# A convolution block with a pooled gate: the gate's second product on VectorE, and the order of work at two stage seams

## The chip, the cores and the metric

The kernel runs on one core of a Trainium2 chip, as one launch. The metric is the device time of the launch in microseconds (us), taken as the median of several runs. Besides, one execution was recorded by the hardware profiler; all views of the profile come from that one.

## The reference, cut to what matters

The input is x, 16 images of 192 channels and 64 by 64 pixels, in fp32. Layer 0 is a convolution block, layer 1 a convolution whose taps depend on the image:

```
h     = layernorm over channels(x)
p, g  = split(conv1x1(h))                       # 192 + 192 channels
p     = depthwise 3x3(p)
mixed = (four directional scans(p) + depthwise 3x3(p)) * sigmoid(g)
mixed = gelu(batchnorm over images and pixels(mixed))
x     = x + conv1x1(mixed)
x     = x + fc2(gelu(fc1(layernorm(x))))        # 192 -> 768 -> 192

t     = mean over pixels(x) @ w1.T              # squeeze: 192 -> 48
t     = relu(gamma * (t - running_mean) * rsqrt(running_var + 1e-5) + beta)
taps  = t @ w2.T + b2                           # excite: 48 -> 192 x 9, of which 4 are kept by a mask
out   = per image and channel 3x3 convolution(x, taps) + bias
```

## The kernel before

The work goes through three stages, each over all images, and every engine's instructions run in the order in which the program writes them (a manual schedule). Most tiles hold two images: image 0 on partitions 0 to 63, image 1 on 64 to 127, with the 192 channels as three tiles t of 64.

**Stage one** (loop over n, eight parts for each of eight image pairs; `project`, `turn`, `variance`) normalises x and projects it. A part has four groups of 128 pixels of each image; four parts fill a block, whose results lie in an SBUF buffer (`stg` for even blocks, `mid` for odd ones). VectorE takes image 0's projection out of PSUM (L520), ScalarE image 1's (L521). The block before is stored by DMA while the next is computed: `store_first` (L530) copies the first group of eight channels by DMA straight into `pg_even`, a part of the SBUF tile `low`, and `store` puts the rest into DRAM (`pg_d`), from the SP and POOL queues. Small preparations are hung beside certain parts n with `beside`, among them `squeeze_scale` (n = 50) and the loads of the later weights (`load_weights`, n = 40 to 44). After the loop, L595 and L596 store the last block's first group and part 0.

**Stage two** (L768, loop over k, one channel of each half at a time, groups of four k's) works on one group of eight channels after the other. Iteration k issues, in this order: the decay tables of k + 1 on ScalarE (`tables`), the vertical products and the gate of k - 1 (`vertical`, `gate`), loads for later groups, the scans of k + 1 on VectorE (`scans`), the depthwise products of k + 2 (`depthwise`), and the local products and sigmoid of k (`local`, `sigmoid`). Iterations -2 and -1 fill the pipeline. In iteration -2 also stands `hidden_bias` (L138): 18 products of one column that add fc1 applied to the second layernorm's bias onto fc1's own bias `bf1`. Its weights `wf1` are scaled by `scale_hidden` in iterations 1, 3 and 5.

**The seam behind stage two** (L801 to L807): `keep_up(4)` and `keep_up(1)` are products whose result nobody reads, which fill TensorE's time; `spread` and `batch_norm` make the batch statistics from VectorE's per-channel statistics; `turn_back` transposes the first mixed chunk for stage three.

**Stage three** (L1257, loop over n, 64 chunks of 512 pixels of an image pair, eight chunks per pair) does the output projection, the MLP and the dynamic convolution. fc2 is computed in seven partial products over halves (`seven`, called by `second`); `first` does fc1 and ScalarE its GELU. Chunk n also prepares chunks n + 1 and n + 2. When a pair has ended (`ended`, at the first chunk of the next one), `pooled` sums what the additions into the image have accumulated. `squeeze` (L1112) then multiplies by `w1t` (three products, 48 outputs for the two images) and applies the batch norm and the relu on VectorE (`red`). Later in the same chunk `excite` (L1122) multiplies `red` by `w2t` with 24 products of one column into `ps_k`, and VectorE adds b2 (`taps`). In the profile each fp32 product is recorded as two, so these are 6 and 48 there. The taps then scale shifted images in `dynamic`: one ScalarE and three VectorE operations per piece, spread over the next chunks. The last pair's pieces follow the loop, as the tail (from L1344 on), partly as diagonal products on TensorE (`dynamic_last`). PSUM tiles of a name tag share a fixed number of buffers: "f1" has two, and holds fc1's results, the output projection's pair (`ps_o`), squeeze's result (`ps_t`) and two of fc2's partial sums (`ps_s`).

Two lines that a sentence doesn't say well, the layout of the pooled sums, in which each half has a column of its own and zeros in the other's, and excite's products:

```
nc.vector.tensor_reduce(pool2[q, :, i], s["sums"][q], AX.X, ALU.add)
both(pk[:, t, k], lambda i: w2t[:, k, 64 * t:64 * t + 64], lambda i: s["red"][:, i:i + 1], True, True)
```

Of the kernel before, what the change touches and what calls it, by code (L numbers as in the profile page):

```python
# [21 lines left out]
F32 = mybir.dt.float32  # L22
AF = mybir.ActivationFunctionType
ALU = mybir.AluOpType
# [31 lines left out]
def conv_block_kernel(ctx: ExitStack, tc: tile.TileContext, x, prm, w_in, w_out, w_fc1, b_fc1, w_fc2, w1, bn1, w2, out):  # L56
# [46 lines left out]
    w2t = k2.tile([RED, NTAP, C], F32, tag="w2t", name="w2t")  # L103
    b1 = k2.tile([RED, 4], F32, tag="b1", name="b1")
    s1 = k2.tile([RED, 1], F32, tag="s1", name="s1")

    mean64 = k2.tile([128, 64], F32, tag="mean64", name="mean64")

    def load_weights(k):

        if k == 0:
            nc.gpsimd.memset(mean64, 1.0 / C)
            nc.sync.dma_start(wo, w_out[0:128])
            for q in HALF:
                nc.sync.dma_start(wo2[q], w_out[128:C])
        elif k == 1:
            load_cls3(wf1, w_fc1)
        elif k == 2:
            nc.sync.dma_start(wf2, w_fc2.rearrange("(m p) c -> p m c", p=128))
        elif k == 3:  # L120
            nc.sync.dma_start(bf1, b_fc1)
            load_cls3(w1t, w1)
            nc.sync.dma_start(w2t, w2[:, 0:NTAP, :])
        else:
            nc.sync.dma_start(b1, bn1)
            nc.sync.dma_start(pv[:, 0], prm[0:128])
            for q in HALF:
                nc.sync.dma_start(pv[q, 1], prm[128:C])


    def squeeze_scale():
        nc.scalar.activation(s1, b1[:, 3:4], AF.Sqrt, bias=eps5[0:RED])
        nc.vector.reciprocal(s1, s1)
        nc.vector.tensor_mul(s1, s1, b1[:, 0:1])

        nc.vector.tensor_scalar_mul(w1t, w1t, 1.0 / NPIX)

# [28 lines left out]
    ones = ce.tile([128, 128], F32, tag="ones", name="ones")  # L166
    pv = ce.tile([128, 2, NPRM], F32, tag="pv", name="pv")
# [11 lines left out]
    mats[0]["lm"] = lm_even  # L179
    mats[1]["lm"] = mid[:, NPG:NPG + 5 * HW * (GC // 2)].rearrange("p (k m c) -> p k m c", k=5, m=HW)  # L180
# [69 lines left out]
    with ExitStack() as stage:  # L250
# [284 lines left out]

        def store(blk, d, queues):
# [58 lines left out]
        store_first(blk)  # L595
# [3 lines left out]
    with ExitStack() as stage:  # L599
# [168 lines left out]
        for k in range(-2, n_bp + 1):  # L768
            if 0 <= k + 1 < n_bp:
                tables(k + 1)  # L770
# [14 lines left out]
            if k == -2:  # L785
                hidden_bias(psb.tile([128, 2, CH], F32, tag="l", name="pb_h")[:, 0])
            if k + 2 < n_bp:
                depthwise(k + 2)
            if 0 <= k < n_bp:
                local(k)  # L790
                sigmoid(k)
            if k in (1, 3, 5):
                scale_hidden(k // 2)
            if k == n_bp - hp_:

                load_y(0, y_low, (nc.sync,), (0, 1))
# [4 lines left out]
        keep_up(4)  # L801
# [4 lines left out]
        batch_norm()  # L806
        turn_back(y_low, mxs[0], 0, 2)  # L807
# [304 lines left out]
    def squeeze(p):  # L1112
        s = pst[p]
        pt = ps2.tile([128, 2, CH], F32, tag="f1", name="ps_t", bufs=2)[:, 0]
        for t in range(3):
            nc.tensor.matmul(pt[0:RED, 0:2], w1t[:, t], pool2[:, t], start=(t == 0), stop=(t == 2))
        red = hp2.tile([RED, 2], F32, tag="red2", name="red2")
        nc.vector.tensor_scalar(red, pt[0:RED, 0:2], b1[:, 2:3], s1, ALU.subtract, ALU.mult)
        nc.vector.tensor_scalar(red, red, b1[:, 1:2], 0.0, ALU.add, ALU.max)
        s["red"] = red  # L1120

    def excite(p):  # L1122
        s = pst[p]
        pk = ps2.tile([128, 3, NTAP, 1], F32, tag="a", name="ps_k")
        for t in range(3):
            for k in range(NTAP):
                both(pk[:, t, k], lambda i: w2t[:, k, 64 * t:64 * t + 64], lambda i: s["red"][:, i:i + 1], True, True)
        taps = hp2.tile([128, 3, NTAP], F32, tag="taps", name="taps")
        nc.vector.tensor_add(taps, pk[:, :, :, 0], pt3[:, :, B2:B2 + NTAP])
# [127 lines left out]
    for n in range(n_ch + 1):  # L1257
# [79 lines left out]
        if ended is not None:  # L1337
            excite(ended)
            if ended < n_pairs - 1:
                pieces += [(ended, g, t) for g in range(NG) for t in range(3)]  # L1340
# [79 lines left out]
```

## Time and profile before

| what | us |
|---|---|
| three runs, median (lowest to highest) | 3562.65 (3562.14 to 3562.84) |
| the profiled execution's own time | 3559.31 |
| its span, first to last instruction | 3557.5 |
| TensorE busy (products) | 3525.5 |
| VectorE busy | 2741.6 |
| ScalarE busy | 1834.7 |
| GpSimd busy | 1155.7 |
| stage one ends on TensorE at | 591.2 |
| stage two's last products end at | 1261.4 |
| tail begins (last pair's squeeze) at | 3520.4 |

In the profile PE is TensorE's products, PEld its weight loads, DVE is VectorE, ACT ScalarE, POOL GpSimd and SP SyncE. A line such as "592.30 4.79 PE L141 MATMUL pb_h<-pt,wf 64*128 64x1 f32 x36 [1.10 <-ACT mid L521]" of the timeline gives the start and the length in us, the engine, the line of the kernel, the operation, what it writes and reads, the size of the weights (rows * columns), the size of the moving operand, the number of instructions, and in brackets how long the engine was idle before and what ended that. In the chain of waits a line gives start, length, engine, tile, line and number. PEclk is the share of TensorE's full clock that was granted. The mean of it is 0.995 over the span.

### The profile page before, as it was taken

The page shows a single profiled execution, that of the slowest core. Times are in us where ns is not written, and L with a number is a line of the kernel's source. Part 1 is how long each engine was busy: PE and PEld are TensorE (multiplying, and loading weights), DVE is VectorE, ACT ScalarE, POOL GpSimd, SP SyncE. Part 2 cuts the span into 40 slices and gives each one's busy share as a digit, 9 for nine tenths or more (in the row PEclk, how much of TensorE's full clock was granted, in tenths as well). Part 3 has the DMA queues.
Part 4 walks back from the last instruction along what each step waited for, and adds up shares of the span by engine and source line. Part 5 has one row for each costly group of instructions (what it writes and reads, how often), then busy time and mean ns, then how long its engine had stood idle before and what let it go on. Part 6 is the DMA issues. An engine that isn't in the chain of part 4 may idle for free.

```text
span 3557.5 us, 79074 instructions
## 1 busy us (share of the span) xinstructions
PE 3525.5 (99%) x33426; PEld 1874.6 (53%) x33426; DVE 2741.6 (77%) x4722; ACT 1834.7 (52%) x2067; POOL 1155.7 (32%) x1246
## 2 busy tenths in 40 slices
PE   9999999999999999999999999999999999999998
PEld 6666866555555544454444444444445444444443
DVE  7888776999999975557777776777677777767765
ACT  3444445888888844344444445454444444453543
POOL 3434342111111134333333333343433333343433
PEclk9999999999999999999999999999999999999999
DMA  7999998999999941112222222222222222232213
GB/s 177 263 272 264 271 294 282 282 301 283 280 282 286 247 123 34 40 54 60 69 71 70 67 65 81 58 75 62 80 60 69 68 74 62 68 82 58 75 34 90
DMA packets 288987, 492.29 MB, mean 138 GB/s; under 512 B 24816, under 2 KB 183016, under 8 KB 288632
## 3 DMA queue, kind: packets, MB, share of 16 engines
q1 hardware_dynamic: 246772, 341.85, 35.8%
q0 software_dynamic: 40928, 144.36, 14.2%
q8 instruction: 263, 4.31, 0.5%
q10 hardware_dynamic: 932, 1.03, 0.1%
q14 instruction: 92, 0.75, 0.1%
HBM read 284.95 MB, written 197.92 MB: 136 GB/s over the span
## 4 chain that ended last, share of the span: by engine, by line
PE 89%; DVE 1%; DMA 1%; issue 0%; ACT 0%; SPq 0%; ACTq 0%; POOL 0%; DVEq 0%
PE ps_f L997 28%; PE ps_f L852 19%; PE ps_l L674 11%; PE ps_pj L515 7%; PE ps_d L630 7%; PE ps_s L852 7%; PE ps_o L907 5%; PE ps_o L900 2%; PE ps_m L936 1%; PE ps_v L936 1%; PE ps_xt L486 1%; PE ps_k L852 0%; DMA pg_d<-mid 0%; DMA xa<-in_x_dram 0%; DMA mixed_d<-mid 0%
## 5 line engine op out<-in xcount | busy, mean ns | idle before, releaser
L997 PE MATMUL ps_f<-h,wf 64*64 64x512 f32 x9216 | 1014.9, 590 | 0.0
L999 ACT ACTIVATE gl<-ps_f,bf 128x1024 f32<-128x1024 f32 x384 | 427.8, 1114 | 1082.3 <-PE ps_f L997 1080.0
L997 PEld LDWEIGHTS ps_f<-h,wf 64*64 64x64 f32 x9216 | 346.2, 133 | 599.0 <-issue 575.1
L852 PE MATMUL ps_f<-gl,place 128*64 128x256 f32 (+1 forms) x3072 | 528.7, 486 | 1.1 <-ACT rs L979 1.1
L515 PE MATMUL ps_pj<-wi,xa 64*128 64x384 f32 x3072 | 520.1, 488 | 9.2 <-DVE stg L520 6.2
L515 PEld LDWEIGHTS ps_pj<-wi,xa 64*128 64x128 f32 x3072 | 334.0, 189 | 159.9 <-DVE stg L520 10.5
L1032 POOL TENSOR_TENSOR gl<-gl 128x512 f32<-128x512 f32 x192 | 308.6, 1634 | 159.2 <-PE ps_f L852 159.0
L852 PEld LDWEIGHTS ps_f<-gl,place 128*64 128x64 f32 x3072 | 225.2, 137 | 217.7 <-issue 145.8
L1022 POOL COPY turn<-o 128x1 f32<-128x1 f32 x84 | 16.4, 195 | 832.8 <-DVE o L65 832.8
L1028 POOL TENSOR_TENSOR t<-gl 128x512 f32<-128x512 f32 x192 | 246.0, 1281 | 89.0 <-ACT gl L999 44.6
L1030 POOL TENSOR_TENSOR t<-gl,t 128x512 f32<-128x512 f32 x192 | 247.0, 1287 | 44.2 <-ACT gl L999 30.8
L65 DVE SCALAR_TENSOR_TENSOR o<-ximg,taps,o 128x1024 f32<-128x1024 f32 x180 | 231.8, 1288 | 4.9
L473 POOL DMA_DIRECT2D xa<-in_x_dram x192 | 120.2, 634 | 323.8 <-PE ps_pj L515 277.1
L665 DVE TENSOR_TENSOR_SCAN v<-tab,q 128x1024 f32<-128x1024 f32 x96 | 218.3, 2274 | 7.8 <-ACT tab L653 7.8
L667 DVE TENSOR_TENSOR_SCAN v<-tab,q 128x1024 f32<-128x1024 f32 x96 | 217.5, 2266 | 0.0
L1055 DVE SCALAR_TENSOR_TENSOR ximg<-ps_f,pt,ximg 128x256 f32<-128x256 f32 (+1 forms) x176 | 96.6, 549 | 151.2 <-PE ps_f L852 151.2
L653 ACT ACTIVATE tab<-mask,dec_b 128x1024 f32<-128x1024 f32 x192 | 209.6, 1144 | 0.0
L521 ACT ACTIVATE mid<-ps_pj,rsa 128x384 f32<-128x384 f32 x128 | 119.5, 937 | 167.0 <-PE ps_pj L515 150.1
L521 ACT ACTIVATE stg<-ps_pj,rsa 128x384 f32<-128x384 f32 x128 | 119.2, 935 | 162.6 <-PE ps_pj L515 144.2
L913 DVE SCALAR_TENSOR_TENSOR ximg<-ps_o,pt,low 128x256 f32<-128x256 f32 x264 | 113.0, 478 | 93.0 <-PE ps_o L907 90.3
L907 PE MATMUL ps_o<-low,wo 128*64 128x256 f32 x1536 | 182.1, 385 | 0.4 <-ACT low L880 0.4
L493 DVE BATCH_NORM_STATS2 st<-ps_xt 128x6 f32<-128x192 f32 x512 | 171.7, 335 | 8.3 <-PE ps_xt L486 7.7
(258 smaller groups left out, 5604.0 us busy)
## 6 DMA issues: line engine op xcount, KB each, us to landing
low<-in_x_dram SPq DMA_DIRECT2D x128, 384.0 KB
out_dram<-o SPq DMA_DIRECT2D x172, 256.0 KB
mid<-pg_d SPq DMA_DIRECT2D x8, 4096.0 KB
low<-mixed_d SPq DMA_DIRECT2D x116, 256.0 KB
low<-pg_d SPq DMA_DIRECT2D x7, 4096.0 KB
pg_o<-pg_d SPq DMA_DIRECT2D x7, 4096.0 KB
xa<-in_x_dram POOLq DMA_DIRECT2D x192, 128.0 KB, 5.6
xa<-in_x_dram SPq DMA_DIRECT2D x192, 128.0 KB
```

What stands on the lines that cost most here:

```text
L65: nc.vector.scalar_tensor_tensor(o, in0, scalar, in1, ALU.mult, ALU.add, **kw)
L515: nc.tensor.matmul(ps[i], pixels(n, t, g)[q], wi[q, t].rearrange("p g k c -> p (g k c)"), start=(t == 0), stop=(t == 2))
L521: nc.scalar.activation(stag[blk][1][:, :, j], ps[1], AF.Copy, scale=rs[:, g, 1:2])
L630: nc.tensor.matmul(dst(ps[o, ih]), mats[g % 2]["dm"][q, di + 1, :, ch], src(s["pg"][q, :, 0, ch]), start=(di == 0), stop=stop)
L674: nc.tensor.matmul(dst(bst[k]["ps"][o, i]), lm_of(g)[q, m, :, c], src(q, ih), start=start, stop=stop)
L852: nc.tensor.matmul(ps[q], w(i), rhs(i), start=start, stop=stop, **kw)
L907: nc.tensor.matmul(ps[wh][q].rearrange("p (r w) -> p r w", w=32), wo[:, 64 * t:64 * t + 64], cols(rows(s["mx"][:, i]))[:, :, wh], start=fi ...
L997: nc.tensor.matmul(pf[o, i], wf1[q, t, m0:m0 + 64], s["h"][q, t], start=(t == 0), stop=(t == 2))
L999: nc.scalar.activation(gl, pf, AF.Gelu, bias=bf1[:, m:m + 1])
L1028: sub(t1[:, m], b12(m), b11(m))
L1030: sub(t2[:, m], b22(m), t1[:, m])
L1032: sub(b12(m), b22(m), b12(m))
```

## The change

Four things change:

- **Excite on VectorE.** `w2t` no longer is a tile of its own: it is loaded late (iteration 92 of stage two, by the POOL queue) into the buffer of the even groups' depthwise matrices, and at the seam behind stage two 24 products against an identity turn it into `w2x`, which has channels on the partitions and the 48 hidden values along the row (`taps_by_channel`; two ScalarE copies out of PSUM). One filler product of `keep_up(4)` goes. The batch norm of the squeeze is folded into `w1t` and a constant `c0` beforehand (four small VectorE operations in `squeeze_scale`, a product and two VectorE operations in `squeeze_rows` behind `batch_norm`). `squeeze` then makes, for each half, the hidden vector on all 64 partitions, with the pooled sum spread over 64 weight columns and `w1t` moving, six products; VectorE adds `c0`, multiplies relu of that by `w2x` over 576 elements, reduces them to 12 and adds b2. All of it stands where squeeze stood; `excite` is gone.
- **The last block's first group by engines.** Behind stage one's loop, `keep_first` copies it with two VectorE and two ScalarE instructions instead of four DMAs; three filler products of 384 columns stand before.
- **Tables first.** The decay tables of channel 0 are made in iteration -2 instead of -1, ahead of the first depthwise results on ScalarE.
- **The MLP bias** (`hidden_bias`) moves from iteration -2 to iteration 0, behind the local products, and uses a PSUM buffer of tag "d".

```diff
-    w2t = k2.tile([RED, NTAP, C], F32, tag="w2t", name="w2t")
+    w2x = k2.tile([128, 3, NTAP, RED], F32, tag="w2x", name="w2x")
+    c0 = k2.tile([128, RED], F32, tag="c0", name="c0")
...
             load_cls3(w1t, w1)
-            nc.sync.dma_start(w2t, w2[:, 0:NTAP, :])
...
         nc.vector.tensor_scalar_mul(w1t, w1t, 1.0 / NPIX)
+        nc.vector.tensor_mul(sq_s, b1[:, 2:3], s1)
+        nc.vector.tensor_sub(sq_s, b1[:, 1:2], sq_s)
+        for k, v in enumerate((s1, sq_s)):
+            nc.vector.tensor_scalar_mul(sq_d[:, k], ident[0:RED, 0:RED], v)
+
+    def squeeze_rows(pr):
+
+        nc.tensor.matmul(pr[:, 0:2 * RED], ones[0:RED], sq_d.rearrange("p k r -> p (k r)"), start=True, stop=True)
+        nc.vector.tensor_mul(w1t, w1t, pr[:, 0:RED].unsqueeze(1).broadcast_to([128, 3, RED]))
+        nc.vector.tensor_copy(c0, pr[:, RED:2 * RED])
+
+    def taps_by_channel(pk):
+
+        for t in range(3):
+            for k in range(NTAP):
+                j = (2 * t + k % 2) * RED
+                for q in HALF:
+                    nc.tensor.matmul(pk[q, k // 2, j:j + RED], w2t[:, k, 64 * t:64 * t + 64], ident[0:RED, 0:RED],
+                                     start=True, stop=True)
+        for h in range(2):
+            nc.scalar.activation(w2x[:, :, 2 * h:2 * h + 2], pk[:, h, 0:6 * RED].rearrange("p (t k r) -> p t k r", t=3, r=RED),
+                                 AF.Copy)
...
+    w2t = mats[0]["dm"][0:RED].rearrange("p k m c -> p (k m c)")[:, 0:NTAP * C].rearrange("p (k c) -> p k c", k=NTAP)
...
+        def keep_first(blk):
+
+            for i, par, q, i8, b, qh in each(blk):
+                o, a = pg_even[qh, i8 * NB + b].rearrange("p k c j -> p (k c) j"), stag[blk][i][q, 0:2 * GC]
+                if i == 0:
+                    nc.vector.tensor_copy(o, a)
+                else:
+                    nc.scalar.activation(o, a, AF.Copy)
...
-        store_first(blk)
+        warm_ = bank()
+        for _ in range(3):
+            nc.tensor.matmul(warm_[:, 0:2 * C], ident, wi[:, 0].rearrange("p g k c -> p (g k c)"), start=True, stop=True)
+        keep_first(blk)
         store(blk, 0, (nc.gpsimd, nc.gpsimd))
...
         for k in range(-2, n_bp + 1):
-            if 0 <= k + 1 < n_bp:
+            if k == -2:
+                tables(0)
+            elif 0 < k + 1 < n_bp:
                 tables(k + 1)
...
-            if k == -2:
-                hidden_bias(psb.tile([128, 2, CH], F32, tag="l", name="pb_h")[:, 0])
             if k + 2 < n_bp:
                 depthwise(k + 2)
             if 0 <= k < n_bp:
                 local(k)
                 sigmoid(k)
+            if k == 0:
+                hidden_bias(psb.tile([128, 2, CH], F32, tag="d", name="pb_h", bufs=2)[:, 0])
...
             if k == n_bp - hp_:
 
+                nc.gpsimd.dma_start(w2t, w2[:, 0:NTAP, :])
...
-        keep_up(4)
+        taps_by_channel(psb.tile([128, 2, CH], F32, tag="d", name="pk_h", bufs=2))
+        keep_up(3)
...
         batch_norm()
+        squeeze_rows(psb.tile([128, 2, CH], F32, tag="d", name="pr_h", bufs=2)[:, 0])
...
         for t in range(3):
-            nc.tensor.matmul(pt[0:RED, 0:2], w1t[:, t], pool2[:, t], start=(t == 0), stop=(t == 2))
-        red = hp2.tile([RED, 2], F32, tag="red2", name="red2")
-        nc.vector.tensor_scalar(red, pt[0:RED, 0:2], b1[:, 2:3], s1, ALU.subtract, ALU.mult)
-        nc.vector.tensor_scalar(red, red, b1[:, 1:2], 0.0, ALU.add, ALU.max)
-        s["red"] = red
-
-    def excite(p):
-        s = pst[p]
-        pk = ps2.tile([128, 3, NTAP, 1], F32, tag="a", name="ps_k")
-        for t in range(3):
-            for k in range(NTAP):
-                both(pk[:, t, k], lambda i: w2t[:, k, 64 * t:64 * t + 64], lambda i: s["red"][:, i:i + 1], True, True)
+            for i, q in enumerate(HALF):
+                nc.tensor.matmul(pt[q, 0:RED], pool2[q, t, i:i + 1].broadcast_to([64, 64]), w1t[q, t], start=(t == 0), stop=(t == 2))
+        red = hp2.tile([128, RED], F32, tag="red2", name="red2")
+        nc.vector.tensor_add(red, pt[:, 0:RED], c0)
+        prod = hp2.tile([128, 3, NTAP, RED], F32, tag="prod", name="prod", bufs=1)
+        flat = lambda a: a.rearrange("p t k r -> p (t k) r")
+        nc.vector.scalar_tensor_tensor(flat(prod), red.unsqueeze(1).broadcast_to([128, 3 * NTAP, RED]), 0.0, flat(w2x), ALU.max, ALU.mult)
         taps = hp2.tile([128, 3, NTAP], F32, tag="taps", name="taps")
-        nc.vector.tensor_add(taps, pk[:, :, :, 0], pt3[:, :, B2:B2 + NTAP])
+        nc.vector.tensor_reduce(taps.rearrange("p t k -> p (t k)"), flat(prod), AX.X, ALU.add)
+        nc.vector.tensor_add(taps, taps, pt3[:, :, B2:B2 + NTAP])
         s["taps"] = taps
...
-        if ended is not None:
-            excite(ended)
-            if ended < n_pairs - 1:
-                pieces += [(ended, g, t) for g in range(NG) for t in range(3)]
+        if ended is not None and ended < n_pairs - 1:
+            pieces += [(ended, g, t) for g in range(NG) for t in range(3)]
```

More of the change, by code (lines that the diff above doesn't have):

```diff
@@ L166, in conv_block_kernel @@
     ones = ce.tile([128, 128], F32, tag="ones", name="ones")
+    sq_s = ce.tile([RED, 1], F32, tag="sq_s", name="sq_s")
+    sq_d = ce.tile([RED, 2, RED], F32, tag="sq_d", name="sq_d")
     pv = ce.tile([128, 2, NPRM], F32, tag="pv", name="pv")
```

## The prediction

> **What bounds the kernel now.** I read the page first: busy time by engine, then the chain that ended last.
>
> ```profile
> PE 3525.5 (99%) x33426; PEld 1874.6 (53%) x33426; DVE 2741.6 (77%) x4722; ACT 1834.7 (52%) x2067; POOL 1155.7 (32%) x1246
> ```
>
> TensorE is busy for 99% of the span, so a change gains what it takes off TensorE, or what it takes out of the few places where TensorE waits or runs slowly. The change touches three such places. First, the ends of image pairs in the last stage, from the chain in order of time:
>
> ```profile
> 1533.89 5.31 PE ps_f L997 x48
> 1568.62 5.31 PE ps_f L997 x48
> 1605.25 5.31 PE ps_f L997 x48
> ```
>
> The same group of products starts every chunk. A plain chunk lasts 1568.62 - 1533.89 = 34.73 us, the chunk in which a pair has ended 1605.25 - 1568.62 = 36.63. So a pair's end costs 1.90 us of TensorE; there are seven inside the loop (chunks 8, 16 ... 56) and an eighth in the tail. The timeline of TensorE shows where it goes, a plain chunk first:
>
> ```profile
> 1554.23 4.04 PE L852 MATMUL ps_f<-gl,place 128*64 128x256 f32 x24
> 1558.10 1.47 PE L852 MATMUL ps_s<-t,ws 128*64 128x256 f32 x12
> ...
> 1586.32 0.39 PE L1116 MATMUL ps_t<-pool,w1t 128*48 128x2 f32 x5
> ...
> 1589.16 4.10 PE L852 MATMUL ps_f<-gl,place 128*64 128x256 f32 x24
> 1593.19 1.56 PE L852 MATMUL ps_k<-red,w2t 48*64 48x1 f32 x48
> 1594.68 1.52 PE L852 MATMUL ps_s<-t,ws 128*64 128x256 f32 x12
> ```
>
> From ps_f to ps_s it is 3.87 us plain and 5.52 at a pair's end: excite (ps_k) costs 1.65. The other 0.25 is squeeze (ps_t). VectorE beside it, in its timeline:
>
> ```profile
> 1587.29 0.92 DVE L913 SCALAR_TENSOR_TENSOR spare<-ps_o,pt,low 128x256 f32<-128x256 f32 x2
> ...
> 1590.74 0.48 DVE L1055 SCALAR_TENSOR_TENSOR spare<-ps_f,pt,spare 128x256 f32<-128x256 f32 x1 [2.48 <-PE ps_f L852]
> ```
>
> VectorE idles 2.48 us before L1055: room for more work there.
>
> Second, the seam of stages one and two, in TensorE's timeline and in the sums by stretch (columns: length, busy PE, PEld, DVE, ACT, POOL, then PEclk, DMA share, GB/s):
>
> ```profile
> 592.30 4.79 PE L141 MATMUL pb_h<-pt,wf 64*128 64x1 f32 x36 [1.10 <-ACT mid L521]
> 597.02 10.71 PE L630 MATMUL ps_d<-low,dm 64*64 64x512 f32 x120
> ```
>
> ```profile
> 592.24:595.65 3.41, 3.35 (x30) 3.36 (x31) 0.00 (x0) 0.00 (x0) 3.10 (x6) 1.00 0.49 124
> 595.65:599.06 3.41, 3.41 (x20) 2.18 (x23) 0.16 (x1) 0.00 (x0) 0.00 (x0) 0.50 0.98 290
> 599.06:602.48 3.42, 3.42 (x36) 1.79 (x32) 0.00 (x0) 0.00 (x0) 0.45 (x1) 0.50 1.08 381
> 602.48:605.89 3.41, 3.41 (x52) 2.00 (x48) 0.74 (x1) 3.36 (x5) 0.48 (x1) 1.00 1.12 379
> ```
>
> TensorE stops at 591.20, waits 1.10, computes the MLP bias (products of one column), and after 3.4 us of these the clock halves for 6.83 us, into the first depthwise.
>
> Third, the seam of stages two and three:
>
> ```profile
> 1261.39 3.70 PE L759 MATMUL ps_i<-wf,ident 128*128 128x512 f32 x8
> 1264.93 1.60 PE L734 MATMUL pm<-stats,ones 128*128 128x192 f32 x4
> ```
>
> ```profile
> 1268.08:1271.49 3.41, 2.80 (x23) 1.96 (x24) 2.56 (x7) 1.33 (x2) 0.00 (x0) 1.00 0.97 277
> 1271.49:1274.91 3.42, 3.04 (x10) 0.77 (x8) 3.38 (x4) 2.64 (x4) 0.00 (x0) 0.50 0.61 180
> ```
>
> The batch statistics (pm) start the moment four filler products (ps_i) are done, 0.05 us after VectorE's last statistics.
>
> **What the Trainium skill says.** "TensorE: Matmul & The Clock Gate", Part 1: the clock halves after an idle window of about 3.4 us and returns after a busy one, and the windows run freely. The trace agrees (3.41 us steps above) and adds that a window full of one-column products counts as idle; one with 1.3 us of full products in 3.41 (1268.08) did too. "VectorE: DVE Perf Modes", the perf-mode tier table and the errata section: fp32 tensor_tensor and tensor_reduce run at one element per cycle, (N+151)/0.96 ns. The trace: 128x512 took 0.69 us (formula 0.691), the 48-element reduce 0.20 (0.207). "ScalarE: Activation LUTs", What ACT_TABLE_LOAD costs: an ACTIVATE with immediate scale and bias takes 186 + 0.833 N ns; the trace has 0.47 for 256 elements with a bias operand, whose price there is 0.49. "DMA: Bandwidth & Descriptors", Anatomy of one DMA: about 2 us fixed; the last low<-mid stores landed in 2.0.
>
> **Part 1, excite on VectorE.** Removed per pair: 48 ps_k products, 1.65 us of TensorE. Squeeze grows from 6 products of 45 ns (0.25 us) to 12 on 64x64 quarters with 48 columns. The trace has no such product. Bounds: 31 ns (ps_k's 1.49/48) to 45 ns each, 0.37 to 0.54, so +0.12 to +0.29; I take +0.2. Added on VectorE: add from PSUM 0.25 (as L1118, 0.27), the 576-element product 0.84 (L65: 0.776 at 512, 1.288 at 1024, so 1.0 ns an element), the reduce 0.76 (estimate by the formula), the tap add 0.17: 2.0 us in place of 0.5. They start at about 1586.95 and end at 1589.0; queued behind on VectorE are L913 (0.92) and a memset (0.1), until 1590.0. L1055 can't start before 1590.74. So 0.7 us are spare: nothing on the path. Seven ends: 7 x (1.65 - 0.2) = **-10.15 us** (-9.5 to -10.7).
>
> In the tail it is a chain: ps_t at 3520.43 to taps done at 3523.32, 2.89 us. New: products 0.55, then 2.0 of VectorE and some 0.15 of hand-overs, 2.7: **-0.2** (-0.5 to +0.2).
>
> **Part 2, first seam.** Before, from 591.20 to the end of the first depthwise (ACT takes it at 602.50): 11.25 us. After: three fillers of 384 columns (ps_i: 0.885 for 512, so 0.66 each) 2.0 us to 593.2; in their shade the copies: ACT free at 592.24, two of 0.40 to 0.47, done by 593.2; VectorE free at 592.16, two of at most 0.42. Four DMA issues go from POOL's and SP's queues, so what stands behind them moves up by about 1 us. Then depthwise at full clock, 2.61 (later x40 groups): 4.6 us. The bias moves behind local products: 36 at 0.11 us (full clock, 30 in 3.35) are 4.0. Saved so far: 11.25 - 4.6 - 4.0 = 2.65. But the bias, wherever it stands, is a stretch of 4 us of one-column products. By my sum it runs from 603.7 to 607.7 (three depthwise and one local product group behind 593.2); on the trace's own grid the window 602.48 to 605.89 would then be 64% bias, more than the 61% or so of light work that halved the clock at 1271.49. I expect the clock to halve there for two windows, a loss of 3.41: 3.41 - 2.65 = **+0.75 us** (-2.65 if it stays full, +0.8 at worst). Tables first: the scan waited for ACT's table until 605.15, but VectorE was not the limit. Its gate for channel 1 came at 621.66, 2.75 us behind TensorE's 618.91, and at 1246.17 it is 0.13 behind, with no wait of TensorE between. So zero: what VectorE gains there only widens that slack, and without the slack it would be a gain. The bias add on VectorE (0.16) waits for TensorE, with gate 0 queued behind, which waits for later products anyway: zero. Group 1's load on POOL (issued 602.03, 13.8 to land, 615.8) feeds products that began at 618.73; it moves up by 1 us, they by at most 2.65: zero, with 1.2 spare.
>
> **Part 3, second seam.** taps_by_channel puts 48 products of 48 columns in place of one filler: 1.5 to 1.9 us for 0.885, and pm comes later by 0.6 to 1.0, on the path to the first GELU. I take +0.75. The two ACT copies out of PSUM (288 elements, 0.43 each) lie in ACT's 9.75 us of idle time; pm's buffer is free by then. squeeze_rows puts one product and 0.4 us of VectorE ahead of the last transpose (done 1272.57; ACT reads it at 1272.89): at most 0.1. The late w2 load stands in POOL's queue four channels (27 us) before use: zero. The half clock of 1271.49 to 1274.91 cost the first output products 0.93 (8 in 1.98, later 1.05); with everything shifted it may miss them. Half of that, -0.45: together **+0.3** (-0.2 to +1.1). In stage one, four small VectorE operations (0.15 to 0.2 each) join at 480 us; TensorE has two banks a side ahead: zero (to +0.7).
>
> **Sum**: -10.15 - 0.2 + 0.75 + 0.3 = -9.3 us against the profiled execution (span 3557.5, its own time 3559.31). The median of the runs, 3562.65, is 3.3 higher; I take the difference over: **3553.3 us**. A measurement can tell about 0.2% (7.1 us) from no change.
>
> **Rivals.** (a) The clock stays full at the first seam (the bias split between two windows): 2 to 3.4 us better, **3550.5**. For: windows run freely. Against: 4 us covers over 60% of some window in most positions. (b) The wait that takes the place: without ps_k, TensorE comes to ps_s at 1593.2, and if ps_s's banks were those of the output pair it would wait for VectorE's L913 until 1594.46; an end gains 0.25, less 0.2, and the total is +0.5: **3563**. Against: the trace's record of the first ps_s product waits on GpSimd alone, in both kinds of chunk, so it seems to have ps_t's banks. (c) Slower: VectorE's broadcast and reduce are slow, and TensorE waits at each pair's end. It decides once the VectorE line is longer than 0.5 + 2.48 = 3.0 us, and passes the gain at 4.45, that is near 2 us for each 576-element operation (3.5 ns an element; L65 has 1.0 to 1.3). At 4 ns, 5.1 us, it is 7 x 0.65 = 4.5 plus 0.85 from the tail and the seams, slower: **3568**. Against it: every row of fp32 VectorE work above.
>
> **Chances.** Forecast 0.60 (its own range 3551.5 to 3555.5), (a) 0.19, (b) 0.15, (c) 0.06. Faster by over 0.2% (below 3555.5): 0.60 x 0.97 + 0.19 = 0.77; within 0.2%: 0.17; slower 0.06. The range runs from (a)'s lower end, 3549.5, to 3558, where half of the hidden wait of (b) would lie.
>
> **What would show it.** Chunks at a pair's end of 35.2 us against 34.73; ps_s 3.9 us behind ps_f with no wait; VectorE's new line near 2.0 us. Depthwise from 593.2 at full clock, and half a clock near 606. pm near 0.7 us later after ps_l. I am wrong if pair ends stay near 36.6, or if the seams move by more than 3 us.

## The result, and the profile after

The changed kernel takes 3548.71 us (median of 5 runs, 3545.64 to 3550.64); the kernel before, on the same chip, 3562.84. The ratio is 0.9956, 95% interval 0.9942 to 0.9971: 14.1 us faster. The forecast was 3553.3 with a range from 3549.5 to 3558.0, so the sign was right, the gain half as large again as forecast, and the time just below the range. The profiled execution took 3545.64 us (span 3543.9), 13.7 less than the one of before.

The page's line of busy time, and the chain of waits at the same three chunks (start, length, tile):

```profile
PE 3512.8 (99%) x33144; PEld 1905.7 (54%) x33144; DVE 2754.9 (78%) x4738; ACT 1836.2 (52%) x2071; POOL 1156.8 (33%) x1245
```

```profile
1533.02 5.31 PE ps_f L1039 x48
1567.75 5.31 PE ps_f L1039 x48
1602.81 5.31 PE ps_f L1039 x48
```

A plain chunk still lasts 1567.75 - 1533.02 = 34.73 us. The chunk at a pair's end lasts 35.06, not 36.63: 1.57 less, and seven of them 11.0. TensorE's and VectorE's timelines in that chunk:

```profile
1585.34 0.51 PE L1159 MATMUL ps_t<-w1t,pool 64*64 64x48 f32 x12
...
1588.42 4.04 PE L894 MATMUL ps_f<-gl,place 128*64 128x256 f32 x24
1592.29 1.47 PE L894 MATMUL ps_s<-t,ws 128*64 128x256 f32 x12
```

```profile
1585.89 0.21 DVE L1161 TENSOR_TENSOR red<-ps_t,c 128x48 f32<-128x48 f32 x1 [4.68 <-PE ps_t L1159]
1586.13 0.87 DVE L1164 SCALAR_TENSOR_TENSOR prod<-red,w2x 128x576 f32<-128x576 f32 x1
1587.03 0.75 DVE L1166 TENSOR_REDUCE taps<-prod 128x12 f32<-128x576 f32 x1
1587.82 0.17 DVE L1167 TENSOR_TENSOR taps<-taps,pt 128x12 f32<-128x12 f32 x1
...
1589.93 0.49 DVE L1097 SCALAR_TENSOR_TENSOR spare<-ps_f,pt,spare 128x256 f32<-128x256 f32 x1 [1.06 <-PE ps_f L894]
```

From ps_f to ps_s it is 3.87 us, as in a plain chunk, and no wait stands before ps_s. VectorE's new line runs from 1585.89 to 1587.99, 2.1 us, and VectorE still idles 1.06 us before L1097. The first seam on TensorE, with the two stretches that matter (columns as before: length, busy PE, PEld, DVE, ACT, POOL, then PEclk, DMA share, GB/s):

```profile
587.03 2.20 PE L631 MATMUL pb<-wi,ident 128*128 128x384 f32 x6
589.34 8.30 PE L667 MATMUL ps_d<-low,dm 64*64 64x512 f32 x116
...
600.36 4.18 PE L163 MATMUL pb_h<-pt,wf 64*128 64x1 f32 x36
604.47 3.19 PE L711 MATMUL ps_l<-v,low 64*64 64x512 f32 x16
```

```profile
601.74:605.15 3.41, 3.41 (x34) 3.18 (x37) 1.53 (x2) 3.41 (x4) 0.00 (x0) 1.00 1.01 387
605.15:608.56 3.41, 3.41 (x24) 1.12 (x20) 0.79 (x1) 0.93 (x1) 0.00 (x0) 0.50 1.03 421
```

The window 601.74 to 605.15 is 80% bias products, and the clock halves in the next one, for one window. In a second trace of the same kernel (e0 below) the windows fall otherwise: the half clock begins within the bias and lasts for two windows.

```profile
599.71 5.39 PE L163 MATMUL pb_h<-pt,wf 64*128 64x1 f32 x36
```

```profile
602.43:605.84 3.41, 3.41 (x17) 2.91 (x21) 0.20 (x2) 2.99 (x3) 0.00 (x0) 0.50 0.98 365
605.84:609.26 3.42, 3.42 (x20) 1.00 (x16) 0.41 (x1) 0.00 (x0) 0.00 (x0) 0.50 1.03 426
```

At the second seam of the changed kernel's first trace:

```profile
1257.54 1.61 PE L154 MATMUL pk_h<-ident,dm 48*64 48x48 f32 x48
...
1261.76 1.52 PE L771 MATMUL pm<-stats,ones 128*128 128x192 f32 x4
...
1268.46 3.75 PE L1252 MATMUL ps_i<-wf,ident 128*128 128x512 f32 x4 [1.43 <-DVE c L146]
1272.14 1.97 PE L949 MATMUL ps_o<-low,wo 128*64 128x256 f32 x8
```

```profile
1267.34:1270.75 3.41, 2.29 (x3) 1.18 (x4) 3.31 (x9) 3.10 (x3) 0.00 (x0) 0.50 0.74 215
1270.75:1274.16 3.41, 3.41 (x14) 0.88 (x16) 1.39 (x2) 1.95 (x2) 2.98 (x7) 0.50 0.63 170
```

Stage three's four fillers (L1252) now wait 1.43 us for VectorE's copy of `c0`, and then run at half clock.

I cut both profiled spans at the same instructions of TensorE. "Stage two" runs from stage one's last projection to the last local products, with the first seam in it; the second seam from there to stage three's first fc1; "chunks" are the 62 steps between the first and the last ps_v; the tail is what follows.

| stretch, us | before | after | difference | forecast |
|---|---|---|---|---|
| stage one ends at | 591.20 | 587.10 | -4.10 | 0 |
| stage two | 670.26 | 670.67 | +0.41 | +0.75 |
| second seam | 29.29 | 32.11 | +2.82 | +0.3 |
| first fc1 to first ps_v | 16.36 | 16.37 | 0 | 0 |
| chunks | 2165.86 | 2154.85 | -11.01 | -10.15 |
| tail | 84.49 | 82.77 | -1.72 | -0.2 |

So stage one has the largest error, though no instruction of TensorE in it was changed. Below, "the account" is the sum of the other lines, -9.5. Each column is one execution, and in both cases a quick one: the chunks agree to 0.01 us between traces of the same code for them, but the end of stage one moves by some 5 us between traces, stage two and the tail by up to 2 (see the experiments).

### The profile page after: what moved, and what is told of

Same layout as the page of the kernel before. It is cut to its first block, busy times and chain, and to the rows that moved or that the text cites. A ratio compares the mean times of both kernels' runs of the same rounds, so it can differ in the third digit from the quotient of the medians.

```text
span 3543.9 us, 78531 instructions
## 1 busy us (share of the span) xinstructions
PE 3512.8 (99%) x33144; PEld 1905.7 (54%) x33144; DVE 2754.9 (78%) x4738; ACT 1836.2 (52%) x2071; POOL 1156.8 (33%) x1245
## 4 chain that ended last, share of the span: by engine, by line
PE 90%; DMA 1%; DVE 1%; issue 0%; ACT 0%; SPq 0%; ACTq 0%; POOL 0%; DVEq 0%
PE ps_f L1039 28%; PE ps_f L894 19%; PE ps_l L711 12%; PE ps_d L667 7%; PE ps_pj L540 7%; PE ps_s L894 7%; PE ps_o L949 5%; PE ps_o L942 2%; PE ps_m L978 1%; PE ps_v L978 1%; DMA xa<-in_x_dram 1%; PE ps_xt L511 1%; DVE ol L65 0%; PE ps_i L1252 0%; DMA bf<-in_b_fc_dram 0%
## 5 line engine op out<-in xcount | busy, mean ns | idle before, releaser
L1072 POOL TENSOR_TENSOR t<-gl,t 128x512 f32<-128x512 f32 x192 | 247.5, 1289 | 43.6 <-ACT gl L1041 30.3
L1097 DVE SCALAR_TENSOR_TENSOR ximg<-ps_f,pt,ximg 128x256 f32<-128x256 f32 (+1 forms) x176 | 96.7, 549 | 145.6 <-PE ps_f L894 145.6
```

The lines of the kernel that those rows point to most:

```text
L1072: sub(t2[:, m], b22(m), t1[:, m])
```

## Experiments

All differences are between medians, against the kernel before on the same chip (its medians 3561.2 to 3562.6).

**The parts alone.** The changed kernel once more (e0); the excite part without the seam edits (e1); the seam edits without the excite part (e2); and the kernel before with only the load of w2 moved from stage one to late in stage two (e3):

```diff
 e3:
-            nc.sync.dma_start(w2t, w2[:, 0:NTAP, :])
...
+                nc.gpsimd.dma_start(w2t, w2[:, 0:NTAP, :])
                 load_y(0, y_low, (nc.sync,), (0, 1))
```

> The kernel after, unchanged, for a second profile on the chip of the other runs. If the 4 us that stage one gained belong to the change, stage one ends near 587 us here too; if they are chance it may end anywhere from 587 to 592. Total -11 to -15 us against before; pair ends 35.06 us again.

> The kernel after with the first seam put back: DMA copies, bias in iteration -2, tables in iteration -1, no fillers. Left is excite on VectorE with its preparations. My account of the profiles: 7 pair ends save 1.57 us each (-11.0), the tail 0 to -1.8, the second seam costs up to 2.9; in sum -8 to -10 us against before, and chunks at a pair's end of 35.06 us. The rival that most of the gain lies at the first seam expects -4 us or less.

> The kernel before with the first seam's three edits alone (engine copies with fillers, tables first, bias behind local products 0). My account: between 0.5 us slower and 2.6 us faster, as the clock halves for two, one or no windows behind the bias; pair ends stay at 36.63 us. The rival that this seam gives what the forecast missed expects -4 us or more in every profile.

> The kernel before with one edit: the load of w2 is moved from part 43 of stage one (SP's queue) to iteration 92 of stage two (POOL's queue), into the same tile. Rival: the load stands in front of x's loads and costs stage one some 4 us, so stage one ends near 587 us on TensorE and the time falls by 4. My theory: 147 KB in some 500 MB cost nothing, stage one ends anywhere between 587 and 592 from run to run, and the time is within 1.5 us of before.

| run | us | ratio, interval |
|---|---|---|
| e0 | 3547.17 | 0.9958, 0.9946 to 0.9970 |
| e1 | 3548.59 | 0.9961, 0.9949 to 0.9974 |
| e2 | 3562.18 | 0.9998, 0.9990 to 1.0006 |
| e3 | 3561.94 | 1.0003, 0.9995 to 1.0011 |

The seam edits at the first seam are worth nothing that these runs can tell. The excite part brings -12.6 us by the medians, but in its trace chunks, second seam, stage two and tail give only -11.0 + 2.4 + 0.5 - 0.4 = -8.5. That trace has no more to give: its execution was the slowest of its five (3551.02 us, 8.3 below the profiled one of before), and its stage one ends at 591.43, as before. So some 4 us of the medians' difference lie outside the stretches that the excite part edits, this trace doesn't show where, and they are not the load of w2 (e3).

**Same instructions, other addresses.** The change drops one tile (w2t) and adds four, so everything allocated behind them moves: by the addresses that the compiler gave, the input and staging tiles of stage one (xa, stg) by 160 bytes per partition, the large tiles (low, mid) by 576. In e11 the changed kernel gets its new tiles inside one tile of the old size at the old place; in e12 the kernel before gets the new addresses, with w2t among the tiles of stage three.

```diff
 e11:
+    was_w2t = k2.tile([128, NTAP * C], F32, tag="was", name="was_w2t")
+    w2x = was_w2t[:, 0:3 * NTAP * RED].rearrange("p (t k r) -> p t k r", t=3, r=RED)
+    c0 = was_w2t[:, 3 * NTAP * RED:3 * NTAP * RED + RED]
...
-    w2x = k2.tile([128, 3, NTAP, RED], F32, tag="w2x", name="w2x")
-    c0 = k2.tile([128, RED], F32, tag="c0", name="c0")
...
 e12:
-    w2t = k2.tile([RED, NTAP, C], F32, tag="w2t", name="w2t")
...
+    k2.tile([128, 13 * RED], F32, tag="pad2", name="pad2")
...
+    ce.tile([RED, 1], F32, tag="pad_s", name="pad_s")
+    ce.tile([RED, 2, RED], F32, tag="pad_d", name="pad_d")
...
+    w2t = k3.tile([RED, NTAP, C], F32, tag="w2t", name="w2t")
+    nc.gpsimd.dma_start(w2t, w2[:, 0:NTAP, :])
```

> The changed kernel, with its new tiles laid in one tile of the size and at the place of the old w2 tile, so that every tile that stage one uses stands at the address that it has in the kernel before (the input tiles and the staging tiles 160 bytes higher than in the changed kernel, the large shared tiles 576 bytes higher). No instruction differs. My theory: the 4 us that stage one wins in the changed kernel and that none of its edits explains come from these addresses (the input and staging tiles start at a multiple of 64 bytes in the changed kernel, 32 bytes off it in the kernel before), since its waits there are for DMAs; then stage one ends near 592 us here and the time is -9.5 to -10.5 us against the kernel before. Rival: it is something else in the edits, or chance; then stage one ends near 587 and the time is -14.

> The kernel before, with the addresses of the changed kernel for every tile of stages one and two: the w2 tile is replaced by a gap of the size of the new tiles and stands among the tiles of stage three, loaded there on the GpSimd queue; nothing else differs. My theory (addresses): stage one ends near 588 us, not 591 to 597, and the time is 3.5 to 5 us below the kernel before. Rival (the change's own instructions, or chance): no difference, within 1 us. The load in stage three has its data long before the first use at the end of the first pair and costs nothing in both.

e11 took 3551.73 us (ratio 0.9971, 0.9961 to 0.9980), 9.8 below the kernel before; stage one ends at 593.29 in its trace. e12 took 3558.31 (0.9992, 0.9986 to 0.9998), 3.3 below; in its trace stage one ends at 591.54, not near 588 as I had expected. So by the medians 3 to 4 us go with the addresses, in both directions (e11's interval overlaps e0's, and e12's lies just below 1). Which property of them? Four runs with a gap, an unused tile, placed ahead of the parameter tile (32 bytes in e14 and e15) or among the weights (32 bytes in e16), and both on the best version (e18, told below):

```diff
 e14 (before), e15 (after); e19 (before) has 88 in place of 8:
     ones = ce.tile([128, 128], F32, tag="ones", name="ones")
+    ce.tile([128, 8], F32, tag="gap", name="gap")
 e16 (before):
+    k2.tile([128, 8], F32, tag="gap2", name="gap2")
     mean64 = k2.tile([128, 64], F32, tag="mean64", name="mean64")
```

> The kernel before with one unused tile of 32 bytes per partition ahead of the parameter tile of stages one and two: the input tiles and the staging tiles of stage one move up by 32 bytes and now start at a multiple of 64, as in the changed kernel; the large shared tiles stay where they were (32 bytes off a multiple of 64). No instruction differs. If the alignment of the input and staging tiles is what stage one gained from: 3 to 4.5 us below the kernel before, and the loads' queue less busy in 60 to 400 us (49 percent of the engines' time, not 50.6). If the 576 bytes of the large tiles matter, or not alignment but distance between tiles: no difference, within 1 us.

> The changed kernel with the same gap of 32 bytes at the same place: its input and staging tiles go from a multiple of 64 bytes to 32 off one. If their alignment is the cause: 3 to 4.5 us lost, -9.5 to -11 us against the kernel before, stage one ending near 592 us. If the distance (160 and 576 bytes) matters and not the alignment: as the changed kernel, -14.

> The kernel before with a gap of 32 bytes among the weights instead, so that the large shared tiles (the first group's tile, the mixed group's, the images') and the input and staging tiles all start at a multiple of 64. If alignment counts for every tile that DMAs read or write: at least the 3 to 4.5 us of the run with the gap further up, and up to 2 us more, since four of ten staging tiles lie in the large tile. If only input and staging tiles matter: the same 3 to 4.5. If alignment does not matter: no difference.

My theory of these four, alignment to 64 bytes, fell: e14 has it and took 3562.2 us (0.9998, 0.9990 to 1.0006). e15 lost it, 3550.56 (0.9963, 0.9950 to 0.9975), 11.4 below; e16 took 3559.78 (0.9993, 0.9986 to 0.9999), 2.1 below. But the packets of the loads told of something graded, so one more run set the offset within 512 bytes alone:

> The kernel before with an unused tile of 352 bytes per partition ahead of the parameter tile: the input and staging tiles then have the same offset within 512 bytes as in the changed kernel (384 and 448), at other addresses; the large tiles stay. If that offset is what stage one gains from (the packets of the loads took 30.0 ns at 384, 30.8 at 416, 31.3 at 448, 32.2 at 32 in the runs so far): packets near 30 ns, the loads' queue at 49 percent, and 3 to 4 us below the kernel before. If it is the distance between tiles, or the large tiles: packets at 31 to 32 ns and no more than 1.5 us.

e19 took 3558.70 us (0.9990, 0.9983 to 0.9997), 3.9 below, and its stage one ends at 588.22. The view of DMA work between 60 and 400 us has the loads' queue (packets, MB, share of the 16 engines' time) of before, after and e19:

```profile
q1 hardware_dynamic: 39592, 45.22, 50.6%
```

```profile
q1 hardware_dynamic: 39557, 45.14, 48.9%
```

```profile
q1 hardware_dynamic: 39556, 45.18, 49.5%
```

The same data took 1.1 to 1.7 points less of the engines' time. From the trace's records of that queue's 512-byte packets in the same stretch (28,416 in each trace), their mean time, and the end of stage one, by the input tiles' offset within 512 bytes:

| offset of xa | kernels | ns a packet | stage one ends at, us |
|---|---|---|---|
| 384 | after, e12, e19 | 30.0, 30.1, 30.2 | 587.1, 591.5, 588.2 |
| 384 | the other nine traces | 29.7 to 30.3 | 586.5 to 591.4 |
| 416 | e15 | 30.8 | 590.9 |
| 448 | e18 | 31.3 | 590.4 |
| 64 | e14, e16 | 31.4, 31.1 | 591.7, 594.6 |
| 32 | before, e2, e3, e11 | 32.4, 32.3, 31.7, 32.0 | 591.2, 592.2, 596.8, 593.3 |

At 384 stage one ends at 588.7 on average (twelve traces), at 32 at 593.4 (four): 4.7 us apart, but single traces overlap. Through stage one the queue has 49,152 such packets, as many as SyncE's 192 loads of xa make (128 KB each, 256 packets), so they are the input loads. The packets alone don't order the kernels' times: e14 and e16 share an offset and differ by 2.4 us, and e18 at 31.3 ns is no slower than e10 at 29.9. What is shown is 384 against 32.

In stage one TensorE waits for inputs that DMAs load and for VectorE's copies into the staging tiles, which are stored by DMAs before they are written again. By the view of waits these sum to 15.0 us in the trace of before (6.3 on xa, 8.7 on stg and mid) and 12.5 in that of after (5.8 and 6.7). But e12 and e1, with the new addresses, wait 15.4 and 15.8; over all traces the mean is 13.3 at offset 384 and 15.5 at 32. So these waits are where part of the 4 us may lie. Why a packet is dearer at one offset was not tried. The staging tiles shift along with xa, so whether their place matters too stays open.

**The slack on VectorE at a pair's end.**

```diff
 e6:
-        nc.vector.scalar_tensor_tensor(flat(prod), red.unsqueeze(1).broadcast_to([128, 3 * NTAP, RED]), 0.0, flat(w2x), ALU.max, ALU.mult)
+        for _ in range(4):
+            nc.vector.scalar_tensor_tensor(flat(prod), red.unsqueeze(1).broadcast_to([128, 3 * NTAP, RED]), 0.0, flat(w2x), ALU.max, ALU.mult)
```

> The product of 576 elements on VectorE at each pair's end is issued four times in place of once (the same value again): three more of some 0.76 us, 2.3 us more of VectorE at each of the seven pair ends, and on the last pair's. My theory: in the changed kernel VectorE idled 1.06 us in the same chunk and the squeeze's line of 2.1 us lies beside TensorE's products, with the next need of what it delays more than 3 us away; so the 62 chunks take as long as in the changed kernel (2154.9 us, within 1 us) and only the last chunk's tail may lose up to 2.3 us: -12 to -14 us against the kernel before. Rival (my case of a VectorE line that is too slow): the slack is only what the idle shows, 1.06 us, so each pair end loses 2.3 - 1.06 = 1.2 us, seven of them 8.7 us: about -5 us against the kernel before. Third: no slack at all, 7 x 2.3 = 16 us: slower than before by 2 us.

It took 3558.45 us (0.9991, 0.9982 to 0.9999), 4.1 below. The chunks took 2161.30 us, 6.45 more than the changed kernel's: 0.92 for each end, for 3 x 0.795 = 2.39 us more of VectorE. So the slack was 2.39 - 0.92 = 1.47 us; my theory of 3 us fell, and the rival's 1.06 was near. TensorE's timeline shows where it is late, one group of products behind the place that I had watched:

```profile
1598.27 1.52 PE L894 MATMUL ps_s<-gl,place 128*64 128x256 f32 x12 [0.70 <-DVE spare L1097]
```

**The second seam.**

```diff
 e5:
         taps_by_channel(psb.tile([128, 2, CH], F32, tag="d", name="pk_h", bufs=2))
+        squeeze_rows(psb.tile([128, 2, CH], F32, tag="d", name="pr_h", bufs=2)[:, 0])
         keep_up(3)
...
         batch_norm()
-        squeeze_rows(psb.tile([128, 2, CH], F32, tag="d", name="pr_h", bufs=2)[:, 0])
 e10, e18 besides:
-        keep_up(3)
+        keep_up(2)
```

> One part altered: the product that spreads the squeeze's scale over the partitions, and VectorE's multiply and copy that read it, stand right behind the products of the tap weights, ahead of the three fillers and the turning back of y, not behind the batch norm. My theory: at the second seam of the changed kernel the fillers of stage three waited 1.43 us for VectorE's copy, the last reader of this product's bank, and then ran at half clock; so the wait goes, the fillers start near 0.3 us behind the last fc-independent work as in the kernel before, and the second seam takes 29.5 to 30.5 us, not 32.1: -16 to -16.5 us against the kernel before. Rival: the time at the second seam is set by the batch norm and the GELU on VectorE and ScalarE, and the fillers only fill it; then the seam stays at 31.5 to 32.1 us and the time at the changed kernel's -14.

> The changed kernel with the product and the two VectorE steps that spread the squeeze's scale moved ahead of the fillers at the second seam, and two fillers there in place of three; the hidden bias stays where the change puts it, behind the local products of k = 0. My theory: the earlier order alone took the second seam from 32.1 to 30.2 us, and with one filler fewer (0.55 us) it took 29.5 us in the run where the bias was spread; so 29.5 here too, first seam as in the changed kernel, the 62 chunks 2154.9 us: about -16 us against the kernel before, 2 us better than the changed kernel. Rival: with less light work on TensorE ahead of the batch norm the clock halves once more, and the time is that of the changed kernel, -14.

> The version with the early squeeze scale and two fillers, with two gaps of 32 bytes, so that the large tiles too start at a multiple of 64 and the input and staging tiles remain on one. If alignment counts for the large tiles: 0.5 to 2 us below that version, -15.5 to -17.5 us against the kernel before, the fastest of all. If only the input and staging tiles matter, or alignment doesn't: as that version, -15.

e5 took 3547.85 us (0.9962, 0.9950 to 0.9975). Its second seam is 30.23 us, 1.9 shorter, and stage three's first products stand so:

```profile
1267.76 3.36 PE L1252 MATMUL ps_i<-wf,ident 128*128 128x512 f32 x4 [0.26 <-DVE mv L785]
1271.05 1.08 PE L949 MATMUL ps_o<-low,wo 128*64 128x256 f32 x8
```

The wait for `c0` is gone. e10 took 3546.56 us (0.9958, 0.9943 to 0.9973), its second seam 29.56. e18 (e10 with both gaps) took 3546.37 (0.9951, 0.9939 to 0.9964), second seam 29.54: with e10 the best version found, 15.0 to 15.5 us below the kernel before. Their intervals overlap the changed kernel's; that they beat it by some 2 us rests on the second seam of the traces.

**The hidden bias.** In e4 it is spread, three products at a time, over six iterations (my expectation says twelve, which is wrong; the scaling follows at 15, 17, 19). e9 is e4 with e10's seam; e13 and e17 are e4 with products at k = 0 that nobody reads.

```diff
 e4:
-    def hidden_bias(pb):
-        for m in range(NFC):
+    def hidden_bias(pb, m_):
+        for m in (m_,):
...
-            if k == 0:
-                hidden_bias(psb.tile([128, 2, CH], F32, tag="d", name="pb_h", bufs=2)[:, 0])
+            if 8 <= k < 8 + NFC:
+                hidden_bias(psb.tile([128, 2, CH], F32, tag="d", name="pb_h", bufs=2)[:, 0], k - 8)
...
 e13, e17 besides (17 and 5):
+            if k == 0:
+                keep_up(5)
```

> One part altered: the 36 one-column products of the hidden bias are no longer issued in one run at k = 0 of stage two, but three at a time in the twelve iterations k = 8 to 19, and the scaling of the hidden weights follows at 15, 17, 19. My theory: in the changed kernel the run of 36 products took 4.2 us and halved the clock for one window of 3.4 us right after it, in which a vertical and a depthwise ran at about half pace (some 1.0 us lost). Spread, the products still cost about 4 us in sum, but no window is left that is mostly light work, so that the half-clock window near 605 us is gone and the time is 1.0 us below the changed kernel's: some -15 us against the kernel before on the same chip. Rival: the clock's dip has nothing to do with the bias, a half-clock window stays near 600 us, time as the changed kernel's (-14). Second rival: a product of one column costs more alone among dense work than in a run, since its weight load then isn't hidden: over 1.5 us slower than the changed kernel (-12.5 or less gain).

> The hidden bias spread over k = 8 to 19, the squeeze's scale ahead of the fillers at the second seam, and one filler fewer there (two, not three). My theory adds up: -1.0 from the half-clock window at the first seam, -1.7 to -2.4 from the wait at the second, -0.6 from the filler, on the changed kernel's -14: -17 to -18 us against the kernel before, and the fastest of the four kernels of this set. Rival: the second seam is bound by the batch norm and GELU, then -15; second rival: with one filler fewer the clock halves in the batch norm's wait, and what was won is lost again, -14.

> The hidden bias spread over k = 8 to 19 as in the run that cost 10 us, and 17 products of 512 columns that nobody reads (about 4.1 us) issued at k = 0, where the change has the bias. My theory: spreading cost 10 us since TensorE then reached the end of the first group 2.5 us earlier, GpSimd's store of the mixed group went out at 628.0 in place of 630.5 us and ran beside the loads on SyncE's queue, whose half of the depthwise weights landed at 648.4 in place of 639.1, and TensorE stood 8.4 us and ran on at half clock. With the 4.1 us put back by fillers the store goes out at 630 us or later, the weights land near 640, the wait is gone, and the time is the changed kernel's plus the spread products' own, at most 2 us: -12 to -14 us against the kernel before. Rival: the spread products, their bank and VectorE's twelve small additions cost the 10 us; then it is some 10 + 4 = 14 us slower than the changed kernel, as the kernel before or worse.

> The hidden bias spread as before, with 5 products of 512 columns that nobody reads at k = 0, not 17: the 17 took about 14 us in the run before and not the 4.1 that I had reckoned, some 0.83 us each, so 5 take 4.2 us, what the bias took there in the changed kernel. My theory: TensorE is then as late at the end of the first group as in the changed kernel, GpSimd's store goes out at 630 us or later, and the wait of 8.4 us for the depthwise weights and the half clock behind it are gone; what is left is the spread products' own cost, six times 0.97 us: 5 to 7 us slower than the changed kernel, -7 to -9 against the kernel before. Rival: the wait for the weights comes from something else in the spreading, and stays: -2 to +2.

e4 took 3558.74 us (0.9988, 0.9980 to 0.9996): 10 slower than the changed kernel, where I had expected a gain of 1. e9 took 3556.53 (0.9982, 0.9976 to 0.9989), 6.0 below the kernel before and not 17 to 18. TensorE's timeline of e4 has the cause, and GpSimd's the store that moved, in e4 and then in the changed kernel:

```profile
648.56 5.07 PE L667 MATMUL ps_d<-mid,dm 64*64 64x512 f32 x40 [8.41 <-DMA dm<-dv_d]
```

```profile
628.04 1.71 POOL L759 DMA_DIRECT2D mixed_d<-low  x1 [20.57 <-DVE low L745]
```

```profile
630.52 1.71 POOL L759 DMA_DIRECT2D mixed_d<-low  x1 [18.75 <-DVE low L745]
```

Without the 4.2 us of bias at k = 0 the first group is mixed sooner, its 2 MB store goes out 2.5 us earlier and runs beside SyncE's loads, and half of the next depthwise weights, issued at 622.4, lands at 648.4; in the changed kernel it was issued at 620.4 and landed at 639.1. TensorE waits 8.4 us and comes back at half clock (10.2 us of it); e9 has the same wait, 8.5. The traces are graded: where the store starts 5.6 us behind the issue of that load, the load takes 26.0 us (e4, e9); at 8.5 to 8.7 us 20.4 (e5, e17); at 9.0 us 19.4 (e11); at 9.8 us or more 16.7 to 18.7 (the other fifteen). e17, with five products of 512 columns (4.56 us) at k = 0, took 3552.70 us (0.9971, 0.9962 to 0.9981): the store goes out at 632.1, the weights land 0.2 us before their use, the wait is gone, and what is left against the changed kernel is in the main six times 0.97 us at the spread products. e13 took 3562.22 (0.9999, 0.9991 to 1.0007): its 17 products took some 14 us where I had reckoned 4.1, but the wait was gone there too.

## Why the prediction was right and where it failed

- **Excite, the chunks: right, term for term.** Forecast 1.45 us an end, measured 1.57. Squeeze's twelve products cost only 0.08 us more than the six before (forecast 0.2, range 0.12 to 0.29). VectorE's line is 2.1 us (2.0), nothing on the path; the reduce of 576 elements took 0.75 us, where the prediction had 0.76 by the formula for tensor_tensor. Rival (b) did not come: no wait at ps_s. Rival (c)'s mechanism is real, but its point lies at a line of 2.1 + 1.47 = 3.6 us (e6), not at 3.0 as the idle time of before suggested.
- **First seam: right in size, partly by cancelling errors.** The clock halved because of the bias near 605, as forecast: with dense products in that place (e17) it stayed full. It halved for two windows in three traces with the bias at k = 0 (e0, e6, e15; stage two 672.0 to 672.2 us) and for one in the other six (after, e2, e5, e10, e11, e18; 670.4 to 670.8). The forecast had two, and took the windows' places from one trace; they lie elsewhere in each. One window cost 1.7 us: from the end of the bias to that of the next depthwise group (610.60) TensorE took 6.13 us, in e17 4.43. So the part that I had put at -2.65 came to some -1.3 (0.41 - 1.7): the first depthwise took 3.25 us until ScalarE could take it, not 2.61, the fillers 2.2, not 2.0, and the bias 4.2, not 4.0. That is 1.0 of the 1.3 to 1.4 missing; the rest was not located. Alone these edits gave no difference (e2).
- **Second seam: wrong, +2.8 for +0.3.** The failing term is "squeeze_rows ... at most 0.1". pm came 0.6 us later, as priced (0.75). But the last product's PSUM tile is read by VectorE's copy last, and stage three's fillers can't begin before that; they waited 1.43 us, fell into two half-clock windows (3.75 us, 2.50 before) and held the output projection up to 1272.14. The clock's half-window that I hoped to miss was doubled instead. With this order the seam takes 31.7 to 32.3 us in all nine traces that have it; e5, with the other order, gets 1.9 us back, which shows that the order is the main cause.
- **Tail: -1.7 for -0.2.** Before, a half-clock window of 3.4 us lay in it, at 3524.3; the trace of after has none there (every trace has one at the very end). Where the tail of a changed trace has one (e1, e5, e9, e10, e13), it takes 83.4 to 84.5 us, and without one 82.8 to 83.7; e6, whose edit lengthens the tail, is left out. So with the window the tail gains 0.0 to 1.1 us, of which my -0.2 is a part; what decides whether a window falls there was not tried.
- **Stage one: "zero", and it was -4.** This is the step that failed: I asked only whether the four new VectorE operations cost something, not where the tiles would lie. With the old addresses (e11) the whole change gives -9.8 us, against my -9.3; the rest of its -14.0 goes with the addresses, 3.3 to 4.2 us by the medians of e11 and e12. That the input loads' packets are cheaper at the new offset is measured; how this becomes some 4 us of the kernel is argued only.

So rival (a)'s 3550.5 was nearer by its number than the forecast, for another reason than its own. The account leaves -8.2 to -9.5 us, with or without the tail's window, and e11 lies within 1.6 of it. That the account comes so near to my -9.3 is luck: the second seam's 2.5 us too much are cancelled by 0.9 too little at the chunks, 1.5 in the tail and 0.3 in stage two.

## What to carry to other kernels

A change that adds or drops a tile moves every tile behind it: before a few microseconds are put down to an edit, run the old instructions at the new addresses and the new ones at the old. A stretch whose end differs by 5 us between traces of one kind can't be judged from one trace of each: compare medians, or many traces. Where an engine's idle time is taken for slack, add work until it hurts: the first late consumer may stand one step behind the one watched. Cheap work in a stretch in which loads are only just in time is also what holds a store back; taking it away can cost more than it took.

## What the runs showed that I had not expected

- DMA packets of 512 bytes took 29.7 to 32.4 ns by the offset of their tile within 512 bytes; between offsets 384 and 32 the whole kernel differed by 3 to 4 us.
- The time of one DMA load depended on when another queue's store began: 26.0 us with a 2 MB store 5.6 us behind its issue, 16.7 to 18.7 with one 9.8 us or more behind (e4, e9 against the other traces).
- Three one-column products among dense ones (six in the profile) cost 0.97 us, 0.32 each (e4, e13, e17); 18 in one run (36 in the profile) took 4.18, 0.23 each.
- A window of TensorE's clock with 2.29 us of dense products in 3.41 (67%, from 1267.34 in the changed kernel) at half clock was followed by another at half clock; one with 80% of one-column products at full clock, in which TensorE was never idle, by a halved one.
